# A last feed-forward block rebuilt by tiles of 128 rows, and other buffer counts for V and K

## The chip, the cores and the metric

The kernel runs on one core of one Trainium2 chip. The metric is the device time of one execution in microseconds (us). Lower is better. Engines are named as the profile names them: PE is TensorE (matrix products), PEld its weight loads, DVE is VectorE, ACT is ScalarE, POOL is GpSimd, and SP is SyncE, which here only issues transfers (DMAs).

## The reference

One transformer layer with the norms after the additions, on x of shape (4, 2048, 256) in 32-bit floats: attention with 16 heads of 16, then a gated feed-forward (256 to 704 and back) whose weights and inputs are rounded to a 4-bit format in blocks of 16.

```python
def attn(x):                       # 16 heads of 16; weights Wq, Wk, Wv, Wo
    q, k, v = (split_heads(x @ W.T) for W in (Wq, Wk, Wv))
    p = softmax(einsum('bhld,bhmd->bhlm', q, k) / 4)
    return merge(einsum('bhlm,bhmd->bhld', p, v)) @ Wo.T

def fp4_quant_dequant(t):          # last dim in blocks of 16
    scale = maximum(max(abs(t)) / 6, 1e-12)
    return nearest_of([0, .5, 1, 1.5, 2, 3, 4, 6], abs(t / scale)) * sign(t) * scale

def fp4_linear(t, w):
    return fp4_quant_dequant(t) @ fp4_quant_dequant(w).T

def ffn(x):
    h = silu(fp4_linear(x, w_gate)) * fp4_linear(x, w_up)
    return fp4_linear(h, w_down)

x = layernorm(x + attn(x))         # no learned scale or shift, eps 1e-5
x = layernorm(x + ffn(x))
```

## The kernel before

**Blocks, steps and periods.** The 4 x 2048 rows are 16 blocks of 512 rows (4 batches of 4). For each block the 16 heads are 4 groups, so there are 64 steps (block, group). A step runs over the 16 tiles of 128 keys of its batch, so there are 1024 periods `n` in the main loop (from line 707). Each period writes, in this order: a piece of row maxima for a step 20 periods ahead (`maxima`, with `LEAD` = 20: products `pm`, reduced by DVE at line 409), the scores and exponentials of its own key tile (`exponentials`: products `pe`, ACT at line 443 into tiles `e`), and the products with V of two periods ago (`values`, into `av`). Then `period` writes one part of a queue of side work: projections of the next batch, preparing the feed-forward weights, and the feed-forward of finished blocks. So the feed-forward of a block is spread over the attention of the next one. The last block has no next one: its feed-forward is written by the loop `while urgent or queue or due` (lines 745 and 746), after all attention.

**The order on the engines.** TensorE's products keep the order in which they are written (`keep_in_program_order`, lines 134 and 137). The instructions of the other engines, and the transfers of SP, are ordered when the program is built: a planner goes through what is ready by its own estimate of times, earlier-written work first. On the chip every engine then keeps its planned order and waits where an input is late.

**Feed-forward** (`feed_forward`, line 597). The residual product `py` of each 128-row tile is copied out of PSUM by ACT (`read`, line 142), added on POOL (line 525) and normed (`layer_norm`: statistics on DVE, the rest on POOL). Two tiles at a time are rounded to fp4: `fp4` (line 145) puts the block maxima, the reciprocal and the exponent mask on DVE, and scaling and rounding on POOL (lines 155, 157, 163 to 165). Then come transposes (`ptq`), the gate and up products (`pg`, `pu`, 352 columns each), tanh and copies on ACT, three elementwise operations per half (lines 549, 550, 563), `fp4` of the hidden tile of 704 columns, transposes (`pth`), down products (`pz`, 128 columns each), addition on POOL (line 594), the second norm, and the store (line 632). In the last block alone the odd tiles' elementwise work is on DVE (line 623). `later` holds steps back by whole periods, and `turned` waits for two tiles at a time.

**V** (line 345). Per block of 512 rows there are four products `pv`. ACT copies each into one of two tiles `vt`, two products to a tile, and after each pair SP writes four stores, one for each head group, to `vx` in DRAM (line 358).

**K** (`load_k`, line 377). Every step loads 4 key blocks as 2 tiles each from DRAM, into a ring of 20 tiles, so two and a half steps. Written at line 727, the load of key block kb for the step two ahead stands right after the exponentials that were the last to use that key block in the present step.

## Time and profile before

| | |
|---|---|
| three runs | 3671.81, 3674.7 and 3677.18 us, median 3674.7 |
| the profiled execution | 3676.19 us, of which the span from first to last instruction is 3674.4 us |
| busy share of the span | PE 96%, DVE 76%, ACT 73%, POOL 35% |
| PE busy, 0 to 400 us | 346.5 of 400 us |
| PE busy, 400 to 3400 us | 2966.1 of 3000 us |
| PE busy, 3400 to 3580 us | 172.7 of 180 us |
| PE busy, 3580 to 3675 us | 50.5 of 95 us |
| transfers | 328.41 MB, mean 89 GB/s |

The last attention product ends at about 3581 us, and the last block's transposed heads (`oT`) are complete at 3584.6 us. What follows is the last feed-forward alone. The times in the views are microseconds from the start of the span. In a list of instructions the columns are start, duration, engine, line and operation, output and inputs with shapes, how many were merged into the line, and in square brackets how long the engine had been idle before and what it waited for. In a list of waits they are the sum, the number of waits and the longest.

### The profile page before, as it was taken

What the parts mean: (1) busy time and instruction counts of PE and PEld (TensorE: products, weight loads), DVE (VectorE), ACT (ScalarE), POOL (GpSimd) and SP (SyncE); (2) the same over time, 40 slices, a digit from 0 to 9 for tenths busy, and PEclk for the clock granted to TensorE, in tenths of its full rate; (3) what the DMA queues carried; (4) which work ended last, traced back from release to release, by engine and by line L of the source; (5) the groups of instructions that cost most, each with busy time, mean ns of one, the idle gap of its engine ahead of it and who ended that gap; (6) DMA issues with size and microseconds to landing.
All of it is one profiled execution on the core that took longest, in us unless ns stands there. A gap on an engine that the chain in (4) does not pass through costs nothing.

```text
span 3674.4 us, 57830 instructions
## 1 busy us (share of the span) xinstructions
PE 3535.7 (96%) x21396; PEld 1598.0 (43%) x21396; DVE 2805.1 (76%) x3250; ACT 2692.1 (73%) x5452; POOL 1292.8 (35%) x1542
## 2 busy tenths in 40 slices
PE   7889999999999999999999999999999999999995
PEld 4333444444444444444444444444443434444343
DVE  4777878777787878778787787877778788878824
ACT  3667777777777777777777777777777777777772
POOL 1340423424243242424324253343424325241525
PEclk9999999999999999999999999999999999999997
DMA  6543323323232322323233232332322222222100
GB/s 207 176 128 100 106 75 106 99 75 111 80 95 91 106 82 84 115 68 115 84 91 100 85 101 79 100 92 70 115 79 59 75 81 59 73 68 87 47 7 6
DMA packets 192146, 328.41 MB, mean 89 GB/s; under 512 B 25848, under 2 KB 69752, under 8 KB 191864
## 3 DMA queue, kind: packets, MB, share of 16 engines
q1 hardware_dynamic: 190472, 323.39, 28.7%
q8 instruction: 171, 2.80, 0.3%
q10 hardware_dynamic: 1392, 1.31, 0.1%
q14 instruction: 111, 0.91, 0.1%
HBM read 237.04 MB, written 86.51 MB: 88 GB/s over the span
## 4 chain that ended last, share of the span: by engine, by line
PE 82%; DVE 12%; POOL 3%; DMA 2%; ACT 1%; issue 1%; SPq 0%; POOLq 0%; ACTq 0%; DVEq 0%
PE av L134 24%; PE pe L134 18%; PE pm L134 15%; DVE mx L409 8%; PE pz L134 6%; PE pg L134 5%; PE pu L134 5%; PE pq L134 3%; PE pv L134 2%; PE pth L137 1%; DMA q<-qx 1%; PE pa L137 1%; PE py L134 1%; PE pn L137 1%; DVE amax L149 1%; DVE st L501 1%
## 5 line engine op out<-in xcount | busy, mean ns | idle before, releaser
L409 DVE TENSOR_REDUCE mx<-pm 128x2 f32<-128x1024 f32 x2048 | 2409.1, 1217 | 670.2 <-PE pm L134 665.7
L443 ACT ACTIVATE e<-pe 128x512 f32<-128x512 f32 x4096 | 2217.9, 596 | 678.4 <-PE pe L134 672.7
L134 PE MATMUL av<-e,v 128*32 128x512 f32 x8192 | 1097.1, 607 | 1.4 <-DMA v<-vx 1.4
L134 PE MATMUL pe<-q,k 64*128 64x512 f32 x4096 | 1035.4, 456 | 5.0 <-ACT e L443 4.7
L134 PEld LDWEIGHTS pe<-q,k 64*128 64x128 f32 x4096 | 475.1, 184 | 967.3 <-ACT e L443 853.4
L134 PE MATMUL pm<-k,q 62*128 62x512 f32 x4096 | 804.4, 448 | 69.2 <-DVE mx L409 59.6
L134 PEld LDWEIGHTS pm<-k,q 62*128 62x128 f32 x4096 | 346.5, 185 | 384.2 <-DVE mx L409 177.4
L134 PEld LDWEIGHTS av<-e,v 128*32 128x32 f32 x8192 | 162.1, 108 | 333.1 <-issue 313.2
L549 POOL TENSOR_TENSOR a<-a,g 128x352 f32<-128x352 f32 x124 | 116.1, 936 | 499.6 <-ACT a L548 499.6
L594 POOL TENSOR_TENSOR x<-x,read 128x128 f32<-128x128 f32 x128 | 59.0, 461 | 494.2 <-ACT read L142 494.2
L134 PE MATMUL pz<-wdT,hT 128*128 128x128 f32 (+1 forms) x1536 | 231.2, 293 | 0.0
L163 POOL TENSOR_TENSOR xn<-xn,m 128x704 f32<-128x704 f32 (+2 forms) x104 | 159.6, 1534 | 154.6 <-DVE m L162 136.0
L134 PEld LDWEIGHTS pz<-wdT,hT 128*128 128x128 f32 (+1 forms) x1536 | 191.9, 191 | 45.8 <-ACT e L443 18.2
L563 POOL TENSOR_TENSOR h<-a,u 128x352 f32<-128x352 f32 x124 | 116.1, 937 | 227.0 <-ACT u L562 224.6
L525 POOL TENSOR_TENSOR x<-x,read 128x256 f32<-128x256 f32 x64 | 46.7, 730 | 400.4 <-ACT read L142 400.2
L134 PE MATMUL pg<-wgT,xqT 128*128 128x352 f32 x512 | 187.0, 488 | 0.0
L134 PE MATMUL pu<-wuT,xqT 128*128 128x352 f32 x512 | 185.2, 484 | 0.0
L164 POOL TENSOR_TENSOR xn<-xn,m 128x704 f32<-128x704 f32 (+2 forms) x104 | 159.9, 1538 | 5.7
L165 POOL TENSOR_TENSOR xn<-xn,sc 128x704 f32<-128x704 f32 (+2 forms) x104 | 131.5, 1264 | 7.8
L550 POOL TENSOR_TENSOR a<-a,g 128x352 f32<-128x352 f32 x124 | 118.9, 958 | 9.7
L134 PEld LDWEIGHTS pg<-wgT,xqT 128*128 128x128 f32 x512 | 88.2, 191 | 58.4 <-ACT e L443 19.2
L134 PEld LDWEIGHTS pu<-wuT,xqT 128*128 128x128 f32 x512 | 87.7, 189 | 58.4 <-ACT e L443 20.0
(95 smaller groups left out, 2277.3 us busy)
## 6 DMA issues: line engine op xcount, KB each, us to landing
k<-kx SPq DMA_DIRECT2D x1024, 128.0 KB
v<-vx SPq DMA_DIRECT2D x64, 768.0 KB
q<-qx SPq DMA_DIRECT2D x256, 124.0 KB
kx<-khi SPq DMA_DIRECT2D x64, 256.0 KB
qx<-qhi SPq DMA_DIRECT2D x64, 256.0 KB
vx<-vt SPq DMA_DIRECT2D x128, 96.0 KB
xb<-in_L_attn_x_dram SPq DMA_DIRECT2D x16, 512.0 KB
kx<-klo SPq DMA_DIRECT2D x32, 256.0 KB
```

The lines of the kernel that those rows point to most:

```text
L134: tc.keep_in_program_order(nc.tensor.matmul(*args, **kw))
L137: tc.keep_in_program_order(nc.tensor.transpose(*args))
L163: engine.tensor_tensor(xn, xn, m, ALU.add)
L164: engine.tensor_tensor(xn, xn, m, ALU.subtract)
L165: engine.tensor_tensor(xn, xn, sc.unsqueeze(2).to_broadcast([p, nb, FB]), ALU.mult)
L409: nc.vector.tensor_reduce(mx_sb[s][:, t, 2 * i : 2 * i + 2, kb], pm, AX.X, ALU.max)
L443: nc.scalar.activation(e, pe[j], AF.Exp, scale=SCALE)
L525: nc.gpsimd.tensor_add(x1[:, t, :], x1[:, t, :], read(py[:, :D]))
L549: engine.tensor_mul(a, a, g)
L550: engine.tensor_add(a, a, g)
L563: engine.tensor_mul(h[:, cols], a, u)
L594: nc.gpsimd.tensor_add(x1[:, t, cols], x1[:, t, cols], read(pz))
```

## The change

Four edits. First, the last block no longer goes through `feed_forward`. A new `feed_forward_last` is written after the main loop, by tiles of 128 rows in an order written out at its end; all elementwise work and rounding is on DVE (`fp4_at_once`), products are read out of PSUM by DVE where they are added, and POOL keeps only two operations of one column per norm. Gate, sum and product are two DVE operations per half instead of three, the down product is one group of 256 columns instead of two of 128, and rows are stored by 128 instead of 256. Its tiles `a`, `g`, `u` use the ring `e` of the exponentials. Second, its rows of x are loaded at the start of the last step. Third, four tiles `vt` instead of two, and one store for all four groups. Fourth, the K ring has 16 tiles instead of 20. `fp4` and `gated` lose their choice of engine, which only the last block used.

```diff
+E_BUFS = 10
...
+    def fp4_at_once(pool, t, tag, gain=1.0):
+        step = nc.vector
+        p, nb, _ = t.shape
+        amax = pool.tile([p, nb], F32, tag="amax" + tag, name="amax")
+        step.tensor_reduce(amax, t, AX.X, ALU.max, apply_absolute_value=True)
+        sc = pool.tile([p, nb], F32, tag="sc" + tag, name="sc")
+        step.tensor_scalar(sc, amax, gain / 6.0, 1e-12, ALU.mult, ALU.max)
+        rs = pool.tile([p, nb], F32, tag="rs" + tag, name="rs")
+        step.reciprocal(rs, sc)
+        step.tensor_scalar(rs, rs, gain * TIES_DOWN, 1.0, ALU.mult, ALU.mult)
+        xn = pool.tile([p, nb, FB], F32, tag="xn" + tag, name="xn", bufs=3 if tag else 2)
+        step.tensor_tensor(xn, t, rs.unsqueeze(2).to_broadcast([p, nb, FB]), ALU.mult)
+        m = pool.tile([p, nb, FB], F32, tag="m" + tag, name="m", bufs=1)
+        step.tensor_single_scalar(m.bitcast(I32), xn.bitcast(I32), EXPONENT, ALU.bitwise_and)
+        step.tensor_scalar(m, m, 1.0, ROUND, ALU.max, ALU.mult)
+        step.tensor_tensor(xn, xn, m, ALU.add)
+        step.tensor_tensor(xn, xn, m, ALU.subtract)
+        step.tensor_tensor(xn, xn, sc.unsqueeze(2).to_broadcast([p, nb, FB]), ALU.mult)
+        return xn
...
-    vt = [const.tile([P, NG, QT // 2, NP, 3 * DH], F32, tag=f"vt{i}", name=f"vt{i}") for i in range(2)]
+    vt = [const.tile([P, NG, QT // 2, NP, 3 * DH], F32, tag=f"vt{i}", name=f"vt{i}") for i in range(4)]
...
-            v = vt[t // 2]
+            v = vt[(tb * 2 + t // 2) % 4]
...
-                for g in range(NG):
-                    nc.sync.dma_start(vx[b % 2][g, :, t0 : t0 + 2, :], v[:, g].rearrange("p t i c -> p t (i c)"))
+                nc.sync.dma_start(
+                    vx[b % 2][:, :, t0 : t0 + 2, :].rearrange("g p t c -> p g (t c)"),
+                    v.rearrange("p g t i c -> p g (t i c)"),
+                )
...
-            k = p1.tile([P, QB], F32R, tag="k", name="k", bufs=20)
+            k = p1.tile([P, QB], F32R, tag="k", name="k", bufs=16)
...
-
-            engine = nc.vector if last and t % 2 else nc.gpsimd
...
+    def load_last(b, qb):
+        x1 = p1.tile([P, QT, D], F32, tag="x1", name="x1", bufs=2)
+        nc.sync.dma_start(x1, x[b, qb * QB : (qb + 1) * QB, :].rearrange("(t p) d -> p t d", p=P))
+        return x1
+    def feed_forward_last(b, qb, x1):
+        heads = [oTs[(b * NQB + qb) * KC + c] for c in range(KC)]
+        xqT = p1.tile([P, KC, QB], F32, tag="xqT", name="xqT")
+        xq, gates, hq, hT, norms = {}, {}, {}, {}, {}
+        def wide(name):
+            return p1.tile([P, QB], F32, tag="e", name=name, bufs=E_BUFS)
+        def moments(t):
+            st = p2.tile([P, 6], F32, tag="st", name="st")
+            nc.vector.bn_stats(st, x1[:, t, :])
+            mv = p2.tile([P, 4, 2], F32, tag="mv", name="mv")
+            nc.vector.bn_aggr(mv[:, 0, :], st)
+            rstd = p2.tile([P, 2], F32, tag="rstd", name="rstd")
+            nc.gpsimd.tensor_scalar_add(rstd[:, :1], mv[:, 0, 1:2], LN_EPS)
+            nc.gpsimd.tensor_tensor(rstd[:, :1], rstd[:, :1], minus_half[:, :1], ALU.pow)
+            norms[t] = mv, rstd
+        def normed(t):
+            mv, rstd = norms.pop(t)
+            nc.vector.tensor_scalar(
+                x1[:, t, :], x1[:, t, :], mv[:, 0, 0:1], rstd[:, :1], ALU.subtract, ALU.mult
+            )
+        def attended(t):
+            py = psum("py")
+            for c in range(KC):
+                matmul(
+                    py[:, :D], heads[c][:, t * P : (t + 1) * P], woT[:, c, :], start=(c == 0), stop=(c == KC - 1)
+                )
+            nc.vector.tensor_add(x1[:, t, :], x1[:, t, :], py[:, :D])
+            moments(t)
+        def quantized(t):
+            normed(t)
+            xq[t] = fp4_at_once(p2, x1[:, t].rearrange("p (b f) -> p b f", f=FB), "")
+        def up(t):
+            pt = psum("ptq")[:, : KC * P].rearrange("p (k n) -> p k n", k=KC)
+            for kc in range(KC):
+                transpose(pt[:, kc, :], xq[t].rearrange("p b f -> p (b f)")[:, kc * P : (kc + 1) * P], ident)
+            nc.scalar.copy(xqT[:, :, t * P : (t + 1) * P], pt)
+            gates[t] = []
+            for half in range(2):
+                cols = slice(half * FH, (half + 1) * FH)
+                pg, pu = psum("pg"), psum("pu")
+                for bank, w in ((pg, wgT), (pu, wuT)):
+                    for kc in range(KC):
+                        matmul(
+                            bank[:, :FH],
+                            xqT[:, kc, t * P : (t + 1) * P],
+                            w[:, kc, cols],
+                            start=(kc == 0),
+                            stop=(kc == KC - 1),
+                        )
+                a, g, u = (wide(name)[:, :FH] for name in "agu")
+                nc.scalar.activation(a, pg[:, :FH], AF.Tanh, scale=0.5)
+                nc.scalar.copy(g, pg[:, :FH])
+                nc.scalar.copy(u, pu[:, :FH])
+                gates[t].append((a, g, u))
+        def hidden(t):
+            h = p2.tile([P, FF], F32, tag="h", name="h")
+            for half, (a, g, u) in enumerate(gates.pop(t)):
+                nc.vector.scalar_tensor_tensor(a, a, 1.0, g, ALU.add, ALU.mult)
+                nc.vector.tensor_mul(h[:, half * FH : (half + 1) * FH], a, u)
+            hq[t] = fp4_at_once(p2, h.rearrange("p (b f) -> p b f", f=FB), "h", gain=0.5)
+        def downward(t):
+            if t % 2 == 0:
+                hT[t // 2] = p2.tile([P, 2, NFC, P], F32, tag="hT", name="hT", bufs=1)
+            q, dst = hq[t].rearrange("p b f -> p (b f)"), hT[t // 2][:, t % 2]
+            for c0 in range(0, NFC, 4):
+                pt = psum("pth")
+                for c in range(c0, min(c0 + 4, NFC)):
+                    w = min(P, FF - c * P)
+                    transpose(pt[:w, (c - c0) * P : (c - c0 + 1) * P], q[:, c * P : c * P + w], ident)
+                if c0 == 0:
+                    nc.scalar.copy(dst[:, :4, :].rearrange("p c n -> p (c n)"), pt)
+                    continue
+                for c in range(c0, NFC):
+                    w = min(P, FF - c * P)
+                    nc.scalar.copy(dst[:w, c, :], pt[:w, (c - c0) * P : (c - c0 + 1) * P])
+            pz = psum("pz")
+            for c in range(NFC):
+                w = min(P, FF - c * P)
+                matmul(pz[:, :D], dst[:w, c, :], wdT[:w, c, :], start=(c == 0), stop=(c == NFC - 1))
+            return pz
+        def added(t, pz):
+            nc.vector.tensor_add(x1[:, t, :], x1[:, t, :], pz[:, :D])
+            moments(t)
+        def stored(t):
+            normed(t)
+            at = qb * QB + t * P
+            nc.sync.dma_start(out[b, at : at + P, :], x1[:, t, :])
+        attended(0)
+        attended(1)
+        quantized(0)
+        up(0)
+        attended(2)
+        quantized(1)
+        up(1)
+        hidden(0)
+        attended(3)
+        quantized(2)
+        pz = downward(0)
+        up(2)
+        hidden(1)
+        added(0, pz)
+        quantized(3)
+        pz = downward(1)
+        up(3)
+        hidden(2)
+        stored(0)
+        added(1, pz)
+        pz = downward(2)
+        hidden(3)
+        stored(1)
+        added(2, pz)
+        pz = downward(3)
+        stored(2)
+        added(3, pz)
+        stored(3)
...
+        if n == N - NKT:
+            x1_last = load_last(*steps[-1][:2])
...
-            if sv % NG == NG - 1:
+            if sv % NG == NG - 1 and sv + 1 < len(steps):
...
+    feed_forward_last(*steps[-1][:2], x1_last)
```

More of the change, by code (lines that the diff above doesn't have):

```diff
@@ L143, in read, with fp4 @@
         return t
-    def fp4(pool, t, tag, gain=1.0, engine=None):
+    def fp4(pool, t, tag, gain=1.0):
         p, nb, _ = t.shape
@@ L153, in fp4 @@
         nc.vector.reciprocal(rs, sc)
-        engine = engine or nc.gpsimd
-        engine.tensor_scalar(rs, rs, gain * TIES_DOWN, 1.0, ALU.mult, ALU.mult)
+        nc.gpsimd.tensor_scalar(rs, rs, gain * TIES_DOWN, 1.0, ALU.mult, ALU.mult)
         xn = pool.tile([p, nb, FB], F32, tag="xn" + tag, name="xn", bufs=3 if tag else 2)
-        engine.tensor_tensor(xn, t, rs.unsqueeze(2).to_broadcast([p, nb, FB]), ALU.mult)
+        nc.gpsimd.tensor_tensor(xn, t, rs.unsqueeze(2).to_broadcast([p, nb, FB]), ALU.mult)
         def rounded():
@@ L162, in rounded @@
             nc.vector.tensor_scalar(m, m, 1.0, ROUND, ALU.max, ALU.mult)
-            engine.tensor_tensor(xn, xn, m, ALU.add)
-            engine.tensor_tensor(xn, xn, m, ALU.subtract)
-            engine.tensor_tensor(xn, xn, sc.unsqueeze(2).to_broadcast([p, nb, FB]), ALU.mult)
+            nc.gpsimd.tensor_tensor(xn, xn, m, ALU.add)
+            nc.gpsimd.tensor_tensor(xn, xn, m, ALU.subtract)
+            nc.gpsimd.tensor_tensor(xn, xn, sc.unsqueeze(2).to_broadcast([p, nb, FB]), ALU.mult)
         return xn, later(1, rounded, 4 if tag == "" else 2)
+    def fp4_at_once(pool, t, tag, gain=1.0):
[17 more added lines that the diff above has]
+        return xn
     ident = const.tile([P, P], F32, tag="ident", name="ident")
@@ L441, in exponentials @@
         for j in range(2):
-            e = p1.tile([P, QB], F32, tag="e", name="e", bufs=10)
+            e = p1.tile([P, QB], F32, tag="e", name="e", bufs=E_BUFS)
             nc.scalar.activation(e, pe[j], AF.Exp, scale=SCALE)
@@ L530, in residual, with gated @@
             yield 900
-    def gated(xqT, h, t, engine):
+    def gated(xqT, h, t):
         for half in range(2):
@@ L548, in gated @@
             nc.scalar.activation(a, pg[:, :FH], AF.Tanh, scale=0.5)
-            engine.tensor_mul(a, a, g)
-            engine.tensor_add(a, a, g)
+            nc.gpsimd.tensor_mul(a, a, g)
+            nc.gpsimd.tensor_add(a, a, g)
             yield 1200
@@ L562, in gated @@
             nc.scalar.copy(u, pu[:, :FH])
-            engine.tensor_mul(h[:, cols], a, u)
+            nc.gpsimd.tensor_mul(h[:, cols], a, u)
             yield 1200
@@ L598, in feed_forward @@
         rows = slice(qb * QB, (qb + 1) * QB)
-        last = b == B - 1 and qb == NQB - 1
         x1 = p1.tile([P, QT, D], F32, tag="x1", name="x1", bufs=2)
@@ L621, in gate @@
         def gate(t):
-            engine = nc.vector if last and t % 2 else nc.gpsimd
             h = p2.tile([P, FF], F32, tag="h", name="h")
-            yield from gated(xqT, h, t, engine)
+            yield from gated(xqT, h, t)
             blocks = h.rearrange("p (b f) -> p b f", f=FB)
-            later(1, lambda: hq.update({t: fp4(p2, blocks, "h", gain=0.5, engine=engine)}))
+            later(1, lambda: hq.update({t: fp4(p2, blocks, "h", gain=0.5)}))
         def out_rows(t):
```

## Prediction

> **What bounds the kernel now.** I read the page first (busy shares, the forty slices), then sums by stretch of time, then the waits of the first 120 us, and last the instructions of the final 90 us, engine by engine. Between 400 and 3400 us PE is busy 2966 of 3000 us, so nothing there can be won from other engines; only a new wait could cost something. What is open lies at the two ends.

> The end, as busy time by stretch (the columns after the stretch are its length, then PE, PEld, DVE, ACT, POOL, the granted clock, DMA):

> ```profile
> 3584.65:3608.10 23.45, 5.33 (x22) 4.01 (x22) 6.94 (x18) 2.07 (x5) 16.83 (x24) 0.63 0.00 0
> 3608.10:3624.00 15.90, 15.90 (x49) 9.81 (x48) 4.95 (x10) 6.93 (x16) 8.57 (x9) 0.90 0.00 1
> 3624.00:3640.00 16.00, 2.62 (x12) 2.09 (x12) 12.54 (x15) 2.10 (x5) 12.38 (x11) 0.64 0.00 1
> 3640.00:3656.00 16.00, 13.37 (x71) 10.06 (x69) 13.02 (x22) 5.15 (x14) 8.47 (x9) 0.93 0.00 1
> 3656.00:3667.30 11.30, 10.45 (x56) 9.14 (x56) 1.31 (x3) 2.02 (x7) 4.09 (x8) 0.71 0.08 25
> ```

> No engine is full throughout: POOL, PE, DVE and POOL, then PE take turns, because the work goes in pairs of tiles. The last feed-forward runs from 3584.65 (oT ready) to 3674.4: 89.75 us. Its PE instructions show two of the waits:

> ```profile
> 3602.12 0.69 PE L137 MATMUL ptq<-ident,xn 128*128 128x128 f32 x2 [14.19 <-POOL xn L165]
> 3638.62 1.94 PE L137 MATMUL pth<-ident,xn 128*128 128x128 f32 x8 [9.13 <-DVE xn L165]
> 3640.35 2.16 PE L134 MATMUL pg<-wgT,xqT 128*128 128x352 f32 x4
> 3642.35 1.35 PE L134 MATMUL pu<-wuT,xqT 128*128 128x352 f32 x4
> ```

> The start, as waits up to 120 us and one wait of SP over the whole run:

> ```profile
> ACT vt L354 <- DMA vx<-vt: 19.7, 6, 7.2
> PEld ptx L137 <- ACT vt L354: 6.3, 3, 4.6
> SPq L383 <- PE pe L134: 896.2, 240, 12.4
> ```

> ACT waits until a V store has left its `vt` tile, and PE behind it loses 6.3 us. The third line says that SP already waits for K slots, so K loads are now issued as early as the ring allows.

> [...] with POOL rounding beside it, line 550 took 1.88 us on DVE, 0.53 us at its shortest. [...] after 9.13 us idle, four `pg` took 2.16 us and the following four `pu` 1.35.

> **The tail, priced.** These are DVE's rows for a hidden tile, with little from POOL beside them:

> ```profile
> 3649.47 0.89 DVE L149 TENSOR_REDUCE amax<-h 128x44 f32<-128x704 f32 x1
> 3650.39 0.19 DVE L151 TENSOR_SCALAR sc<-amax 128x44 f32<-128x44 f32 x1
> 3650.61 0.43 DVE L153 RECIPROCAL rs<-sc 128x44 f32<-128x44 f32 x1
> 3651.37 0.89 DVE L157 TENSOR_TENSOR xn<-h,rs 128x704 f32<-128x704 f32 x1
> 3652.18 0.42 DVE L501 BATCH_NORM_STATS2 st<-x 128x6 f32<-128x256 f32 x1
> 3652.51 0.51 DVE L161 TENSOR_SCALAR m<-xn 128x704 int32<-128x704 int32 x1
> ```

> A dependent DVE operation starts about 0.03 us after the one before. The fifth line, a norm's statistics among the rounding, shows that the planner fills DVE's order from other tiles, so I count on it below. For 256 columns I estimate from two sizes of the same row: tensor_tensor 0.89 (704) and 0.53 (352) give 0.43; tensor_scalar 0.52 (704) and 0.43 (512) give 0.31; reduce 0.89 and 0.69 give 0.43.

> Per tile on DVE: residual add 0.43, statistics 0.43 and 0.18, gaps 0.09: 1.13. Norm 0.34. `fp4_at_once` of 256: 0.43 + 0.18 + 0.26 + 0.18 + 0.43 + 2 x 0.31 + 3 x 0.43 = 3.39, with gaps 3.76. Gating, 4 operations of 352 columns at 0.56: 2.24. The fused (a+1)g has no row; it lies between one tensor_tensor (0.53) and the two it replaces (1.06); I take 0.53, the upper end adds 8 x 0.53 = 4.2 us. `fp4_at_once` of 704: 0.89 + 0.19 + 0.43 + 0.19 + 0.89 + 2 x 0.53 + 3 x 0.89 = 6.32, with gaps 6.72. Second add with statistics 1.13, norm 0.34. Sum 15.66 a tile, 62.6 for four.

> Removed with it: POOL's products and most of its 53 us of busy time in the last 95 us[...]; ACT's `read` copies (0.37 and 0.27 us each) leave the path, as DVE reads PSUM directly.

> Is DVE fed? PE needs per tile `ptq` 0.33, 16 gate and up records at 0.295 = 4.7, `py` 0.94, `pth` 1.0, `pz` 12 records at 0.235 (the `py` row, 256 columns) = 2.8: 9.8 us at full clock, about 13 with two cold starts, against DVE's 15.66. It fits, except twice.

> First, at the start. `py` of tile 0 is ready at 3585.25. DVE adds tiles 0 and 1 (2.26), then norms and rounds them (2 x 4.1) until 3595.8. Tile 0's transposes start at 3591.7 on a cold PE: 0.5 + 0.45 for the copy, `pg` 2.55 and `pu` 1.68 as in the cold row of before, two more groups at 1.2, ACT's copy and the last product: gating ends at 3600.3. In these 4.5 us DVE has 2.24 us of work, so 2.3 us idle. The residual product of tile 2 stands behind tile 0's up products in PE's order and comes at 3600.2, just in time.

> Second, the end. Of DVE's 62.6 us, 12.7 are done by 3600.3; 1.47 (tile 3's addition and norm) follow the last product; 1.81 (tiles 1 and 2) fit beside it. The rest, 46.6, ends at 3646.9. Then tile 3 goes down on a cold PE: four transposes 0.98, copy 0.66, twelve `pz` [...]: 5.7 us, to 3652.6. Add and statistics 1.13, POOL's two column operations with hand-overs 1.17, norm 0.34: 3655.3. The store takes what it took before, from the last norm's end at 3671.2 to 3674.4: 3.2. End 3658.5, so the tail gains 15.9 us, say 16. PSUM and the `e` ring (6 tiles of 10 per row tile, freed by gating) hold two row tiles loosely; if a slot is late, ACT's next copy waits and PE behind it, covered by the 9 us of the preceding hidden rounding.

> Other edits. x of the last block loads 16 periods ahead; before it was in time too (POOL's first addition waited for ACT's copy): nothing.

> **V.** The wait on `vt` doubles its distance from one block to two; SP issues 8 stores instead of 32 before 80 us. Those 32 at 0.43 us were 13.8 us of SP; the nearest row for a store of 512 pieces is the load of `xb`, 0.53 each, so 4.2. [...] Of PE's 6.3 us I take 5 as won: maxima on DVE need 48.7 us of this stage's 62, so they don't refill it at once. Bounds: nothing (SP then waits elsewhere), and 12 if SP, freer, also brings the feed-forward weights sooner; DVE waited 23.4 us on them (`wl`), for which PE stood still 4.77, 2.56 and 7.67 us between 120 and 245. Below nothing, 6: those same waits may grow in a new order. From 400 us on PE hides V entirely.

> **K.** With 20 tiles a load may go 8 periods before its place in the program, with 16 only at its place: after the exponentials just before it. That place is 8 periods before the first maxima that need it; a period is (3578 - 98) / 1024 = 3.4 us, so 27 us. Four issues of 0.59 and a landing of 2.7 us (seen at 124.7) need 5. Behind a waiting K load stand V, q and x loads and the row maxima's transfer (`q<-nr`); that transfer is written after a K load whose exponentials are two periods old, so it isn't held. Cost nothing, hidden by 22 us of slack; beyond it, PE pays in full.

> Sum: 3674.4 - 16 - 5 = 3653.4 of span. The profiled execution took 3676.19 and the median is 3674.7, near its span; on the median 3674.7 - 21 = 3653.7, so 3654.

> **Rivals.**
> A, the forecast: tail 16, start 5. 3648 to 3660, chance 0.60.
> B, the planner's order fits badly: one or two up or down passes of about 6 us are exposed because DVE's fixed order waits while PE is cold, or the start gives nothing. Gain 8 to 14: 3660 to 3667. For it: PE's clock in the tail, 0.63 at worst, which an estimate may not know. Against: DVE has work of other tiles. 0.16.
> C, the start gains 10 or more, the `wl` waits shrinking as well: 3640 to 3648. Against: they hang on POOL's rounding too. 0.09.
> D, the change doesn't do what it says: V's wait moves to SP and two to three passes are exposed: 3667.4 to 3682, about the same. 0.07.
> E, slower: K loads come late. Place: the maxima at the start of each key block in the main loop. There are some 250 groups of loads; the gain of 21 us is gone at 0.08 us each, and at 0.11 us (28 us) the kernel is slower by 0.2%. For it: SP's 896 us of waiting on slots. Against: PE shows no DMA wait after 400 us, and 22 us of slack. At 0.15 us: 3691. 0.08.

> Within 0.2%, 7.3 us, a measurement can't tell a change from none. Faster: A, B, C, 0.85; same 0.07; slower 0.08. The range takes A, B and half of C: 3643 to 3667.

> **What would show it.** Right: DVE near full from 3586 to 3647 by the old clock with operations of 0.89 us for 704 columns, PE waiting for DVE and not DVE for PE; no line `ACT vt <- DMA vx<-vt`; PE without `k` waits after 400 us. Wrong: DVE gaps of over 3 us ended by ACT or PE in the tail; `pm` waiting on `k<-kx`; larger `amax <- wl` waits before 300 us.

## The result, and the profile after

The changed kernel takes 3653.54 us (median of five runs, 3651.45 to 3656.40) against 3674.7: a ratio of 0.9942, with a 95% interval from 0.9929 to 0.9956. That is 21.2 us less; the forecast was 3654 us.

In the profiled executions the span falls from 3674.4 to 3649.4 us. "Last heads" below is the moment when the last `oT` is ready (the `py` product that waits for it starts); what follows is the last feed-forward alone. The last column is the changed kernel profiled once more, with the third group of experiments (run 9).

| stretch, us | before | after | after, again |
|---|---|---|---|
| first score product (`pe`) | 98.47 | 88.69 | 91.03 |
| first product with V (`av`) | 106.17 | 99.19 | 102.67 |
| last heads | 3584.65 | 3575.68 | 3581.92 |
| last heads to end | 89.75 | 73.72 | 73.98 |
| span | 3674.4 | 3649.4 | 3655.9 |

The tail is shorter by 16.0 us in the first profile and by 15.8 in the second; 15.9 was forecast. But the tail varies too: eight profiles with this same last block (these two and runs 1, 4 to 7 and 10 below) have 71.84 to 73.98 us, so the gain is 15.8 to 17.9 us. The part before it differs by 9.0 us in one and 2.7 in the other, with the same program: the start varies by several us from execution to execution. With 16.0 us for the tail the medians leave 21.2 - 16.0 = 5.2 us for the start; 5 was forecast.

First the changed kernel's tail by stretch of time (length, then PE, PEld, DVE, ACT, POOL, granted clock, DMA):

```profile
3575.68:3587.00 11.32, 3.77 (x11) 2.37 (x12) 8.19 (x28) 0.37 (x1) 1.61 (x4) 0.76 0.00 0
3587.00:3600.00 13.00, 11.80 (x41) 7.49 (x39) 8.49 (x22) 5.42 (x13) 0.78 (x2) 0.95 0.00 1
3600.00:3613.00 13.00, 9.75 (x29) 6.53 (x30) 10.03 (x29) 2.09 (x6) 2.05 (x4) 0.74 0.00 0
3613.00:3626.00 13.00, 11.46 (x45) 7.06 (x43) 12.02 (x30) 5.06 (x13) 1.93 (x3) 1.00 0.07 22
3626.00:3637.40 11.40, 5.73 (x19) 3.86 (x18) 9.32 (x17) 1.36 (x4) 0.77 (x1) 0.79 0.00 0
```

POOL has all but vanished from the tail (53.0 us of work before, 8.5 after). PE and DVE now work in the same stretches and no longer in turns; only the fourth stretch has DVE nearly full, and it is the one where the clock is whole. PE's instructions in the tail:

```profile
3584.33 0.69 PE L138 MATMUL ptq<-ident,xn 128*128 128x128 f32 x2 [7.08 <-DVE xn L187]
3585.48 2.72 PE L135 MATMUL pg<-wgT,xqT 128*128 128x352 f32 x4 [0.46 <-ACT xqT L720]
...
3602.53 1.51 PE L138 MATMUL pth<-ident,xn 128*128 128x128 f32 x6 [3.27 <-DVE xn L187]
3604.30 5.25 PE L135 MATMUL pz<-wdT,hT 128*128 128x256 f32 x12 [0.25 <-ACT hT L757]
...
3616.00 0.88 PE L138 MATMUL pth<-ident,xn 128*128 128x128 f32 x6 [0.62 <-DVE xn L187]
3617.34 3.05 PE L135 MATMUL pz<-wdT,hT 128*128 128x256 f32 x12 [0.46 <-ACT hT L757]
...
3628.03 0.87 PE L138 MATMUL pth<-ident,xn 128*128 128x128 f32 x6 [1.82 <-DVE xn L187]
3629.42 4.64 PE L135 MATMUL pz<-wdT,hT 128*128 128x256 f32 x12 [0.51 <-ACT hT L757]
...
3637.43 1.54 PE L138 MATMUL pth<-ident,xn 128*128 128x128 f32 x6 [3.37 <-DVE xn L187]
3639.22 4.86 PE L135 MATMUL pz<-wdT,hT 128*128 128x256 f32 x12 [0.25 <-ACT hT L757]
```

The wait of 14.19 us before the first transposes is now 7.08, that of 9.13 before the hidden tiles' transposes is 3.37 or less. But the same twelve `pz` take 3.05 us for tile 1, where PE had hardly been idle, 5.25 and 4.86 for tiles 0 and 3 after some 3.3 us of idling, and 4.64 for tile 2 after 1.82 us. DVE pays for it (its instructions that waited longest after the first gating):

```profile
3609.59 0.42 DVE L769 TENSOR_TENSOR x<-x,pz 128x256 f32<-128x256 f32 x1 [2.98 <-PE pz L135]
...
3634.10 0.42 DVE L769 TENSOR_TENSOR x<-x,pz 128x256 f32<-128x256 f32 x1 [1.81 <-PE pz L135]
...
3644.12 0.42 DVE L769 TENSOR_TENSOR x<-x,pz 128x256 f32<-128x256 f32 x1 [5.57 <-PE pz L135]
```

Only the last of these had been foreseen as exposed. The first two are additions that the planned order put ahead of rounding work which was ready.

Now the waits of the changed kernel's first 120 us:

```profile
ACT vt L375 <- PE pv L135: 16.0, 16, 1.9
...
PE av L135 <- DMA v<-vx: 4.2, 1, 4.2
```

ACT waits for products, no longer for V stores, as the forecast wanted. The first product with V, however, now waits 4.2 us for V's load, 1.4 before.

### The profile page after: what moved, and what is told of

Same layout as the page of the kernel before. It is cut to its first block, busy times and chain, and to the rows that moved or that the text cites. A ratio compares the mean times of both kernels' runs of the same rounds, so it can differ in the third digit from the quotient of the medians.

```text
span 3649.4 us, 57772 instructions
## 1 busy us (share of the span) xinstructions
PE 3534.1 (97%) x21348; PEld 1593.8 (44%) x21348; DVE 2816.2 (77%) x3310; ACT 2691.0 (74%) x5446; POOL 1251.3 (34%) x1496
## 3 DMA queue, kind: packets, MB, share of 16 engines
q10 hardware_dynamic: 1392, 1.31, 0.1%
## 4 chain that ended last, share of the span: by engine, by line
PE 82%; DVE 12%; DMA 2%; POOL 2%; issue 1%; ACT 1%; SPq 0%; POOLq 0%; ACTq 0%; DVEq 0%
PE av L135 24%; PE pe L135 18%; PE pm L135 16%; DVE mx L432 9%; PE pz L135 6%; PE pg L135 5%; PE pu L135 5%; PE pq L135 3%; PE pv L135 2%; PE pth L138 1%; PE pa L138 1%; PE py L135 1%; PE pn L138 1%; DMA qx<-qhi 1%; DVE st L524 1%
## 5 line engine op out<-in xcount | busy, mean ns | idle before, releaser
L572 POOL TENSOR_TENSOR a<-a,g 128x352 f32<-128x352 f32 x120 | 112.6, 938 | 494.5 <-ACT a L571 494.5
L135 PEld LDWEIGHTS pz<-wdT,hT 128*128 128x128 f32 x1488 | 190.5, 193 | 50.5 <-ACT e L466 18.2
L163 POOL TENSOR_TENSOR xn<-xn,m 128x704 f32<-128x704 f32 (+2 forms) x100 | 153.6, 1536 | 153.5 <-DVE m L162 131.6
L164 POOL TENSOR_TENSOR xn<-xn,m 128x704 f32<-128x704 f32 (+2 forms) x100 | 153.8, 1538 | 5.4
L165 POOL TENSOR_TENSOR xn<-xn,sc 128x704 f32<-128x704 f32 (+2 forms) x100 | 126.4, 1264 | 7.5
L573 POOL TENSOR_TENSOR a<-a,g 128x352 f32<-128x352 f32 x120 | 113.9, 949 | 9.4
```

What stands on the lines that cost most here:

```text
L135: tc.keep_in_program_order(nc.tensor.matmul(*args, **kw))
L163: nc.gpsimd.tensor_tensor(xn, xn, m, ALU.add)
L164: nc.gpsimd.tensor_tensor(xn, xn, m, ALU.subtract)
L165: nc.gpsimd.tensor_tensor(xn, xn, sc.unsqueeze(2).to_broadcast([p, nb, FB]), ALU.mult)
L572: nc.gpsimd.tensor_mul(a, a, g)
L573: nc.gpsimd.tensor_add(a, a, g)
```

## The experiments

Three groups, each beside the kernel before on its chip (its medians there: 3675.04, 3675.22 and 3673.95 us). Times are medians; ratios are to the kernel before, with 95% intervals.

| run | median, us | ratio | interval | first `av` | last heads | tail |
|---|---|---|---|---|---|---|
| 1 new tail alone | 3658.65 | 0.9956 | 0.9941 to 0.9971 | 106.98 | 3586.41 | 72.79 |
| 2 V and K alone | 3668.77 | 0.9985 | 0.9976 to 0.9994 | 102.10 | 3576.93 | 89.27 |
| 3 16 K tiles alone | 3674.30 | 0.9999 | 0.9990 to 1.0008 | 104.02 | 3582.47 | 89.53 |
| 4 four V tiles, four stores | 3659.38 | 0.9957 | 0.9942 to 0.9972 | 106.32 | 3582.77 | 73.73 |
| 5 two V tiles, one store | 3653.76 | 0.9942 | 0.9927 to 0.9956 | 100.67 | 3576.56 | 71.84 |
| 6 14 K tiles | 3649.21 | 0.9926 | 0.9909 to 0.9942 | 98.45 | 3577.05 | 72.35 |
| 7 12 K tiles | 4651.14 | 1.2655 | 1.2611 to 1.2698 | 96.30 | 4564.85 | 72.15 |
| 8 idle transposes | 3650.02 | 0.9932 | 0.9917 to 0.9946 | 102.92 | 3582.64 | 68.16 |
| 9 changed kernel again | 3654.10 | 0.9946 | 0.9934 to 0.9959 | 102.67 | 3581.92 | 73.98 |
| 10 four stores from ACT | 3688.11 | 1.0038 | 1.0025 to 1.0050 | 109.07 | 3614.25 | 71.85 |
| 11 more idle transposes | 3648.41 | 0.9931 | 0.9919 to 0.9944 | 102.22 | 3577.36 | 67.34 |
| 12 gating unfused | 3659.51 | 0.9959 | 0.9944 to 0.9975 | 101.61 | 3582.81 | 76.19 |

### 1: the new tail alone

```diff
 # the changed kernel with V and K as before
-    vt = [... for i in range(4)]
+    vt = [... for i in range(2)]
-            v = vt[(tb * 2 + t // 2) % 4]
+            v = vt[t // 2]
-                nc.sync.dma_start(vx[b % 2][:, :, t0 : t0 + 2, :]..., v...)
+                for g in range(NG):
+                    nc.sync.dma_start(vx[b % 2][g, :, t0 : t0 + 2, :], v[:, g]...)
-    k = p1.tile([P, QB], F32R, tag="k", name="k", bufs=16)
+    k = p1.tile([P, QB], F32R, tag="k", name="k", bufs=20)
```

> The kernel before with the new last feed-forward alone (two V tiles, four stores, 20 K tiles as before). If the parts add as the prediction has them, the time falls by 16 us to about 3659, the stretch from the last heads to the end is about 74 us as in the changed kernel (73.7), and the start keeps ACT's waits on V stores (19.7 us). Rival: the new tail depends on what the K and V buffers did to the order, and gives less than 12 us.

16.4 us less than before, and a tail of 72.79 us. Its first 420 us keep the old waits: ACT 19.0 us on V stores. The tail's gain doesn't depend on the other edits.

### 2: V and K alone

```diff
 # the kernel before with
-    vt = [... for i in range(2)]
+    vt = [... for i in range(4)]
...
+    # one store for all groups, 16 K tiles, as in the change
```

> The kernel before with four V tiles, one store and 16 K tiles, old tail. The prediction gives 5 us for this, the changed kernel's profile shows 9 us at the end of attention: expected 5 to 9 us, so 3666 to 3670; the tail stays at about 90 us. Rival: the 9 us are chance of one execution, and the gain is under 3 us.

6.3 us less, with an interval of 2 to 9 us; the tail is the old one. With run 1 that makes 16.4 + 6.3 = 22.7 us for parts that together gave 21.2: they add, within what can be measured.

### 3: 16 K tiles alone

```diff
-    k = p1.tile([P, QB], F32R, tag="k", name="k", bufs=20)
+    k = p1.tile([P, QB], F32R, tag="k", name="k", bufs=16)
```

> The kernel before with 16 K tiles instead of 20 and nothing else. Forecast of the prediction: no change (within 3 us), PE with no waits on K loads after 400 us. Rival E: slower by several us or more. A third view: fewer early K loads leave the transfers of the feed-forward weights room in the first 250 us, and the gain seen beyond 5 us comes from here: faster by 2 to 4 us.

No change: 0.7 us less, the interval from 3.7 us less to 2.9 more. The third view isn't borne out by the time either.

### 4 and 5: which half of the V edit counts

```diff
 # 4: the changed kernel with four stores again
-                nc.sync.dma_start(vx[b % 2][:, :, t0 : t0 + 2, :]..., v...)
+                for g in range(NG):
+                    nc.sync.dma_start(vx[b % 2][g, :, t0 : t0 + 2, :], v[:, g]...)
 # 5: the changed kernel with two tiles again
-    vt = [... for i in range(4)]
+    vt = [... for i in range(2)]
-            v = vt[(tb * 2 + t // 2) % 4]
+            v = vt[t // 2]
```

> The changed kernel with its four V tiles but four stores per pair again. If the distance of reuse is what removes ACT's wait, that wait stays near nothing and the time is that of the changed kernel within 2 us. If SP's 24 extra issues before 80 us matter, ACT waits again for V stores or the exponentials start 3 to 6 us later.

> The changed kernel with two V tiles again and the one store kept. If the distance of reuse is the cause, ACT waits for V stores again (some 10 to 20 us in all before 80 us) and the time is 4 to 7 us over the changed kernel, near 3659. If the number of stores on SP is the cause, the wait is under 5 us and the time is within 2 us of the changed kernel.

Run 4 has no wait of ACT on V stores left, yet its first product with V comes at 106.32 us, where the kernel before has it (106.17). The chain of run 4 in that stretch says why (start, length, what):

```profile
90.62 0.58 SPq L362
91.25 0.79 SPq L362
92.13 2.71 DMA q<-nr
94.97 0.77 PE pe L135
95.77 1.09 ACT e L464 x2
97.34 1.09 SPq L362
98.48 0.61 SPq L362
99.14 1.06 SPq L362
100.25 6.03 DMA v<-vx
106.32 1.92 PE av L135 x5
```

From 42 to 103 us SP issues almost without a break, V's stores until 81.6 us. The row maxima's transfer (`q<-nr`) then stands in its queue behind stores of K and q (line 362), and V's load behind more stores of K. The scores wait for the first, the products with V for the second. Run 5 is the other half. In its first 420 us ACT still waits 12.1 us for V stores, since the tiles come back after one block again:

```profile
ACT vt L375 <- DMA vx<-vt: 12.1, 4, 7.0
...
PEld ptx L138 <- ACT vt L375: 1.4, 4, 0.7
```

PE's share of that has shrunk to 1.4 us, the first product with V comes at 100.67, and the time is that of the changed kernel (3653.76). So one store does without the extra tiles what the whole V edit does. The extra tiles without it give 3659.38, beside 3658.65 in run 1, which has neither, on the same chip. The four times of run 4 spread from 3652.51 to 3663.89, so that the extra tiles gain nothing is likely and not proven. The first product with V sorts all fourteen profiles by the stores: 96.30 to 102.92 us with one, 104.02 to 109.07 with four.

### 6 and 7: how much slack K had

```diff
 # 6, 7: the changed kernel with
-    k = p1.tile([P, QB], F32R, tag="k", name="k", bufs=16)
+    k = p1.tile([P, QB], F32R, tag="k", name="k", bufs=14)    # 7: 12
```

> The changed kernel with 14 K tiles: a load can start only 5 periods (17 us) before its first use instead of 8. Issue and landing need about 5 us, so by the prediction's slack this costs nothing: within 3 us of the changed kernel. Rival E: the slack is smaller than worked out, since SP's queue is in order, and PE shows waits at the key blocks: over 10 us slower.

> The changed kernel with 12 K tiles: a load can start only 1 period (3.4 us) before its first use, less than the 5 us that issue and landing need. By the prediction's reckoning PE pays at about 240 key blocks, 2 to 5 us each: 480 to 1200 us slower. If this too costs little, the maxima are not bound to the load as I think.

With 14 tiles nothing is lost (4.3 us under the changed kernel's first median, with overlapping intervals). PE's waits from 400 to 3400 us are a single line, with no K load in it:

```profile
PE pm L135 <- DVE mx L432: 34.2, 79, 0.8
```

With 12 tiles the kernel is 998 us slower than the changed one, about 4.0 us for each of some 250 groups of loads. Not all of this is the waiting itself: between 400 and 3400 us PE's mean granted clock is 0.92, where the changed kernel has 1.00. The largest of PE's waits over its whole run is on a K load:

```profile
PE pm L135 <- DMA k<-kx: 378.0, 364, 10.9
```

The forecast had reckoned 27 us of lead against 5 needed: 8 periods from the end of the exponentials that free the tiles to the first maxima. Counted in the same way 14 tiles leave 4 periods (14 us) and 12 leave none; the expectations above count one period more. Leads of 27 and 14 us suffice, none doesn't, and the loss is of the size expected (480 to 1200 us).

### 8 and 11: the cold clock

```diff
 # the changed kernel with transposes that nobody reads; 11 has 52, 16, 8 and 20
+        def keep_warm(n):
+            pw = psum("pw")
+            for _ in range(n):
+                transpose(pw[:, :P], ident, ident)
...
         attended(1)
+        keep_warm(26)
         quantized(0)
...
+        keep_warm(12)
         pz = downward(0)
...
+        keep_warm(6)
         pz = downward(2)
...
+        keep_warm(14)
         pz = downward(3)
```

> The changed kernel with idle transposes of the identity (26, 12, 6 and 14) on PE in four gaps of the tail, so that its clock is not halved when the work comes; nothing reads them. If the cold clock is what the tail's remaining gaps come from, the first gate and up pass saves 1.6 us, the down passes of tiles 0, 2 and 3 save 2.5, 1.5 and 2.5: 6 to 8 us in all, the tail goes from 73.7 to about 66 us, and this beats both kernels. Rival: VectorE's fixed order is the bound, and only the last pass shows: 2 to 3 us.

> As the run with idle transposes, but 52, 16, 8 and 20 of them, since 26 took only 3.0 us and left PE idle for 4.3 us before the first gate pass. Cold clock as the cause: the first gate and up pass now saves its 2.6 us as well, the tail comes to 66 us or less, and the median is 5 to 7 us below the changed kernel on this chip. If the first pass stays as it was, 68 us.

The tail falls to 68.16 and 67.34 us, below all eight profiles without the transposes (71.84 to 73.98). Beside run 9 on the same chip, run 11 is 5.7 us lower and their five runs each don't overlap (3646.82 to 3651.49 against 3651.62 to 3657.92). This version beats both kernels. All down passes of run 11 are now short, that of tile 3 among them:

```profile
3578.76 5.84 PE L138 MATMUL pw<-ident 128*128 128x128 f32 x52
3586.09 0.41 PE L138 MATMUL ptq<-ident,xn 128*128 128x128 f32 x2 [1.49 <-DVE xn L187]
3586.96 2.72 PE L135 MATMUL pg<-wgT,xqT 128*128 128x352 f32 x4 [0.46 <-ACT xqT L720]
...
3634.98 0.85 PE L138 MATMUL pth<-ident,xn 128*128 128x128 f32 x6 [1.13 <-DVE xn L187]
3636.29 3.05 PE L135 MATMUL pz<-wdT,hT 128*128 128x256 f32 x12 [0.46 <-ACT hT L757]
```

The last two lines were 1.54 and 4.86 us. The first gate pass stays at 2.72 us all the same; I come back to that below.

### 9: the changed kernel again

> The changed kernel itself, beside the next three on the same chip: about 3653.5 us, between 3650 and 3657; a second execution's profile shows how far the start (88.7 us to the first score, 99.2 to the first product with V) and the tail (73.7) vary by themselves: I expect 1 to 2 us in the tail and up to 6 in the start.

3654.10 us, 0.6 over the first median. The tail differs by 0.3 us between these two profiles (by up to 2.1 over the eight), the start by 3.5 us at the first product with V and 6.2 at the last heads. Differences of a few us at "last heads" in a single profile, such as those between runs 4 and 5, therefore say little.

### 10: the four stores on another queue

```diff
 # the changed kernel with
-                nc.sync.dma_start(vx[b % 2][:, :, t0 : t0 + 2, :]..., v...)
+                for g in range(NG):
+                    nc.scalar.dma_start(vx[b % 2][g, :, t0 : t0 + 2, :], v[:, g]...)
```

> The changed kernel with four stores per pair again, issued by ScalarE's queue and not SP's. If it is SP's issuing that held back the row maxima's transfer and V's load in the run with four stores, the first product with V comes near 99 to 101 us and not at 106, and the time is that of the changed kernel within 3 us (ScalarE has room: 73% busy). If the number of transfers itself costs, wherever issued, the first product with V stays at 105 or later and the time is 4 to 6 us over the changed kernel.

Neither: 3688.11 us, slower than the kernel before. The first score comes at 102.83 us; ACT's own copies of `xT`, which the projections need, waited 10.4 us behind its V stores, so this run doesn't separate SP's issuing from the number of transfers. And between 300 and 3100 us PE is busy 2752.7 of 2800 us against 2769.7 in run 9. In a list of instructions of run 10:

```profile
953.88 0.43 ACT L375 COPY vt<-pv 128x128 f32<-128x128 f32 x2
954.34 0.42 PE L135 MATMUL pe<-q,k 64*128 64x512 f32 x2
954.35 1.78 ACTq L379 DMA_DIRECT2D vx<-vt  x4
954.69 1.07 PE L135 MATMUL av<-e,v 128*32 128x512 f32 x8
...
956.17 2.07 ACT L464 ACTIVATE e<-pe 128x512 f32<-128x512 f32 x4 [1.86 <-PE pe L135]
```

The exponentials of the products at 954.34 start only at 956.17, after four issues of together 1.78 us. ACT is busy for only 73% of the span in the kernel before, yet here its issues hold up work that PE waits for.

### 12: gating unfused

```diff
-                nc.vector.scalar_tensor_tensor(a, a, 1.0, g, ALU.add, ALU.mult)
+                nc.vector.tensor_mul(a, a, g)
+                nc.vector.tensor_add(a, a, g)
```

> The changed kernel with the gating's fused operation taken apart into two, as before: eight more operations of 352 columns on VectorE. If VectorE's chain is what the tail consists of, as the sum has it, this costs up to 8 x 0.53 = 4.2 us of tail: at least 3, since the first two or so fall into its idle time. If PE's passes and hand-overs set the pace, under 1.5 us.

DVE's busy time in the tail rises by 53.48 - 49.90 = 3.6 us, and the tail, 76.19 us, is 2.2 to 4.4 us over the eight profiles with the fused operation. That is more than the 1.5 us of the other answer; whether "at least 3" holds can't be said from one profile. Taken with runs 8 and 11, the tail is neither DVE's chain alone nor the passes of PE alone. (The time, 5.4 us over run 9, contains a start that varies by more than this effect.)

## Why the prediction was right, point by point

**The sum of the tail, right in total, wrong in two terms that cancelled.** By the marks after the last heads, forecast and measured: gating of tile 0 finished 15.7 and 17.3 us; tile 3's rounding finished 62.3 and 61.7; its down pass 5.7 and 6.7 (its twelve `pz`: 4.1, which rests on an estimate of the author's of how long the clock stays halved, shown by no trace, and 4.86 measured); addition, statistics and norm 2.6 and 2.5; the store 3.2 and 2.8; together 73.8 and 73.7. That the total fits to 0.1 us is luck, since the same last block varies by 2.1 us. Inside the first 62 us the step "A dependent DVE operation starts about 0.03 us after the one before", applied to every operation, was the wrong one. The planner mixed the chains of two tiles, and operations that don't depend on their neighbours started 0.08 and 0.09 us before those ended. The changed kernel's DVE in the second half of the tail:

```profile
3617.91 0.42 DVE L186 TENSOR_TENSOR xn<-xn,m 128x256 f32<-128x256 f32 x1
3618.24 0.88 DVE L174 TENSOR_REDUCE amax<-h 128x44 f32<-128x704 f32 x1
3619.04 0.42 DVE L187 TENSOR_TENSOR xn<-xn,sc 128x256 f32<-128x256 f32 x1
3619.37 0.18 DVE L176 TENSOR_SCALAR sc<-amax 128x44 f32<-128x44 f32 x1
```

Operations of 0.42 and 0.88 us start 0.33 and 0.80 us apart. So the tail's DVE work is 49.9 us of busy time and not 62.6. (Of the 62.6 some 0.7 us is also a slip: ten operations at 0.03 us are 0.30 us of gaps for each rounding, where the sum has 0.37 and 0.40.) Against that, its idle time between the first addition and the last norm is 19.7 us. The forecast's own times leave 3655.3 - 3585.25 - 62.6 = 7.45 us. The difference is mainly the first gating, 4.7 instead of 2.3, the additions after tiles 0 and 2's down passes 2.98 and 1.81 instead of nothing, and 0.64 to 0.76 us at each of several norms that wait for POOL. Per-operation durations themselves, 0.42 for 256 columns and 0.52 for the fused operation, came as estimated. Of the signs named for being right, "DVE near full" did not come: it is busy 49.9 of 73.7 us.

**"It fits" for PE, half right.** Up passes never held DVE up after the first tile. Down passes of a cold PE (granted clock 0.50 from 3637.4 to 3641 us, tile 3's) did, which is a mild form of rival B; runs 8 and 11 show it. Against run 9, 5.8 and 6.6 us of tail come back when the clock is kept up in them, and at least 3.7 and 4.5 against any of the eight profiles.

**V: the amount right by luck, the cause not.** The step "The wait on `vt` doubles its distance" was taken as the source of the 5 us. Run 5 has the old distance and the full gain. The second reason named there, SP's 8 issues instead of 32, is the one that the runs favour: the chain of run 4 runs through SP. Run 10 could not separate the issuing from the number of transfers, so that much stays open. The upper bound of 12 through the weights' loads wasn't needed: DVE's waits on `wl` fell from 23.4 to 18.8 us in one profile, and to 19.4 in the next.

**K: right.** Run 3 puts it at nothing, and runs 6 and 7 find the edge between 14 us of lead and none. SP's waits on K slots grew, from 896.2 to 1119.6 us, and PE waited for no K load after 400 us; rival E had taken that line as a warning. The line of the changed kernel's page of SP waits:

```profile
SPq L406 <- PE pe L135: 1119.6, 388, 12.4
```

## What to carry to other kernels

A tail in which engines take turns is shortened by giving one engine a whole small tile's chain and letting other tiles fill its waits; price such a chain by start-to-start distances of mixed work, price separately each pass through an engine whose clock has dropped (here 4.86 us against 3.05 for the same twelve products), and don't judge a change of 2 us in such a tail by one profile. Before shrinking a ring of buffers, compute in us the lead that is left: here 27 and 14 us, against some 5 for issue and landing, cost nothing, and none cost 998 us. Before enlarging a buffer because an engine waits for its store, look at what the queue that issues the store is doing: fewer issues may be the cheaper cure (here 3653.76 us with one store and two tiles, 3659.38 with four of each), and moving them to a compute engine can cost more than they did (3688.11).

## What the runs showed of the hardware that I had not expected

What the traces show is a grid: in all fourteen, every change of the granted clock comes a multiple of 3.41 us after the one before (in the kernel before and the changed one alone, 52 such intervals). Cut along that grid, run 11 before its first gate pass, the changed kernel around tile 2's down pass, and run 5 around the same pass look like this (columns as above):

```profile
3580.01:3583.42 3.41, 3.41 (x34) 3.41 (x32) 2.28 (x11) 0.00 (x0) 1.25 (x3) 1.00 0.00 0
3583.42:3586.84 3.42, 1.59 (x13) 1.14 (x11) 3.25 (x11) 0.31 (x1) 0.00 (x0) 1.00 0.00 0
3586.84:3590.25 3.41, 3.29 (x6) 2.04 (x7) 0.94 (x3) 0.54 (x3) 0.00 (x0) 0.50 0.00 0
...
3625.84:3629.26 3.42, 1.25 (x8) 0.61 (x6) 3.39 (x6) 1.03 (x3) 0.00 (x0) 1.00 0.00 0
3629.26:3632.67 3.41, 3.25 (x8) 2.62 (x9) 2.82 (x7) 0.43 (x3) 0.00 (x0) 0.50 0.00 0
...
3625.06:3628.48 3.42, 1.61 (x7) 0.73 (x6) 3.42 (x6) 1.26 (x3) 0.00 (x0) 1.00 0.11 37
3628.48:3631.89 3.41, 2.90 (x16) 2.31 (x16) 3.20 (x7) 0.90 (x3) 0.00 (x0) 1.00 0.00 0
```

Stretches with PE busy for 1.59 us and 1.25 us were followed by one at half the clock, the stretch with 1.61 us was not. After the last heads, over all fourteen traces, a whole clock fell after each of 43 stretches with PE busy for 1.40 us or less, and held after each of 139 with 1.60 us or more. In between lie two: it held after 1.55 us in run 8 and fell after 1.59 in run 11. So tile 2's down pass met a halved clock in the changed kernel and a whole one in run 5 after gaps of the same length, over which the grid lay differently. Idle transposes do count: the first stretch above holds nothing else on PE (busy 3.41 us), and the next one still has a clock of 1.00. Those of run 11 ended 2.2 us before the second stretch did. The busy share alone doesn't settle it, though: in the changed kernel's attention the clock also fell after stretches with PE busy for 1.89 us (from 2973.90) and 1.88 us (from 3185.52), and why isn't settled here.
